# Routing's order from the last unit but one on, and the weights of both expert layers through four common buffers

## The chip, the core and the metric

The kernel runs on one core of one Trainium2 chip. The metric is the device time of one execution in microseconds (us). Differences are read against the kernel before on the same chip. The core has TensorE (PE, with its weight load PEld), VectorE (DVE), ScalarE (ACT), GpSimd (POOL) and SyncE (SP). In this kernel SP issues nearly all transfers, POOL issues a few, and nothing but SP and POOL issues any.

## The reference, cut to what matters

```python
# x, ctx: (4, 1024, 512) f32; 16 heads of 32
x = x + attention(layernorm(x), ctx, ctx)      # causal mask, softmax, @ Wo.T + bo
n = layernorm(x)                               # the tokens of the second part
grouped = n.reshape(4, 32, 32, 512)            # groups g of 32 tokens t
logits = einsum('bgtd,des->bgtes', grouped, controller) + tie      # 32 x 4 = 128 experts
perm = (logits == max(logits, over t))         # each expert takes one token of each group
disp = einsum('bgtd,bgtes->bgesd', grouped, perm)
inner = relu(einsum('bgesd,desf->bgesf', disp, f1) + bias)         # first layer
y = einsum('bgesf,esfd->bgesd', inner, f2)                         # second layer
x = x + einsum('bgesd,bgtes->bgtd', y, perm)
```

## The kernel before, in words

**Attention.** 16 units (4 batches times 4 chunks of 128 hidden columns, four heads each) run one after the other. Unit `u` has 12 steps `k`. In step `k` the scores of unit `u+1` are formed for their row maxima (`score_piece`, L426, reduced by DVE in L438), and the scores of unit `u` are formed transposed (`key_block`, L492 and L498), exponentiated by ACT (L506), masked by POOL (`affine_select`, L509), summed by DVE and POOL (L525 to L529) and multiplied with the values (`weigh_values`, L542). The sums are gathered on PE (`pd`, L572) and inverted (L579). All but the last inverse go to DRAM and come back spread over the partitions (L583, L586), and L567 multiplies them in. The output product of a batch (`o_step`, L374, with the addition L379) runs in later units. The order is written by a planner: `fill` and `soon` hold PE work, `slot` places it against estimated costs, and `later`/`beside` hold small DVE work, of which `beside(0.9)` takes some in each step. PE, DVE, ACT and POOL execute in the order of this source (`manual_schedule`); SP too in the units after the first. In routing and in the expert layers, SP is left to the scheduler.

**Routing.** The 4096 tokens go through in eight blocks `q` of 512 tokens (four rows of 128). Blocks 0 to 5 belong to batches 0 to 2 and are read back from `x2_dram` (`load_tokens`, 1 MB each). Blocks 6 and 7 are the last batch, whose eight output rows are made here: `last_row` loads the residual, adds the output bias on POOL (`residual`, L344), forms the product in the one buffer of `ps_o` (L911), adds on DVE (L916), stores, and measures the row (L362, L363). A block is normalized (`normalize_row`, L737, four rows, in place), stored to `xn_dram`, turned by PE (`turn_row`, L748), multiplied with the controller (`choose_tokens`, L930; DVE then adds `tie`, takes the maximum and compares, L937 to L942; POOL stores the choice, L944), turned back (`return_choice`, L949) and dispatched to the experts (`dispatch`, L1058, evicted by DVE L1066 and ACT L1068). Block 0 is turned inside the last unit (`turn_first`). Step `n` of the loop (L967) does: two turns of block `n`, the choice of block `n-1`, two turns, load of block `n+2`, normalization and store of block `n+1`, return of `n-2`, dispatch of `n-3`, then the rows of `LAST_ROWS[n-1]` (2, 2, 2, 1, 1, 0, 0).

**Expert layers.** The first layer takes four passes over chunks of 128 columns (`products`, L1115, added up in `inner`) beside the dispatch of the next chunk; its weights `f1` come in 16 transfers of 512 KB through four buffers. The second layer takes four passes `dq` of 128 output columns: eight `second_layer` steps `m` (L1183, weights `f2` in 32 transfers of 256 KB through twelve buffers), 32 turns (L1197), and in the next pass eight `combine` steps (L1208, L1212; loaded rows `xr` in eight buffers, stores issued by POOL in L1213).

The functions that the change touches, with the profile's line numbers:

Of the kernel before, what the change touches and what calls it, by code (L numbers as in the profile page):

```python
# [18 lines left out]
P = 128  # L19
# [5 lines left out]
def attention_phase(  # L25
# [696 lines left out]
    NQ = B * S // (QN * P)  # L722
    LAST = NQ - NT // QN
    LAST_ROWS = (2, 2, 2, 1, 1, 0, 0)
    xn_dram, permT_dram = routed
    tokens, turned = {}, {}

    def load_tokens(q):
        if q < LAST:
            tokens[q] = wpool.tile([P, QN, D], F32, tag=("w_q", "w_k")[q % 2], name=f"x2_{q}")  # L730
            nc.sync.dma_start(
                tokens[q], x2_dram[ts(q, QN * P), :].rearrange("(t p) d -> p t d", p=P)
            )
# [12 lines left out]
    def turn_row(q, i, px):  # L746
        for c in range(NC):
            nc.tensor.transpose(px[:, c, :], tokens[q][:, i, ts(c, P)], ident)  # L748

    def turn_first(i):  # L750
        finish(("rows", 0, i))
# [12 lines left out]
    for u in range(-1, NU):  # L764
# [129 lines left out]
    tie_sb = rpool.tile([P, T], F32, tag="tie", name="tie_sb", bufs=1)  # L894
    nc.sync.dma_start(tie_sb, tie)
    banks = ExitStack()
    ps_o = pool("ps_ro", 1, banks, space=PSUM)
    ps_x = pool("ps_rx", 2, banks, space=PSUM)
# [3 lines left out]
    def last_row(t):  # L902
        q, i = LAST + t // QN, t % QN
        if i == 0:
            tokens[q] = lpool.tile([P, QN, D], F32, tag="x2l", name=f"x2_{q}")
        if t + 1 < NT:
            load_residual(B - 1, t + 1)
        xt = residual(B - 1, t)
        po = ps_o.tile([P, D], F32, tag="po", name=f"po_{B - 1}_{t}")
        for c in range(NC):  # L910
            nc.tensor.matmul(  # L911
                po, lhsT=atTs[(B - 1) * NC + c][:, ts(t, P)], rhs=weights["o"][:, c, :],
                start=(c == 0), stop=(c == NC - 1),
            )
# [37 lines left out]
    def load_first(q):  # L952
# [2 lines left out]
            firsts[q], xn_dram[ts(q, QN * P), ds(0, P)].rearrange("(t p) d -> p t d", p=P)  # L955
        )

    firsts = {}

    for q in range(2):  # L960
        store_tokens(q)
    load_residual(B - 1, 0)
    variances((B - 2) * NT, (B - 1) * NT)
    roots((B - 2) * NT, (B - 1) * NT)
    load_tokens(2)
    row = 0
    for n in range(1, NQ):  # L967
        for i in range(2):
            turn_tokens(n, i)
        choose_tokens(n - 1)  # L970
        for i in range(2, QN):
            turn_tokens(n, i)
        load_tokens(n + 2)
        if 1 < n < LAST + 2:
            load_first(n - 2)
        if n + 1 < NQ:
            for i in range(QN):
                normalize_row(n + 1, i)
            store_tokens(n + 1)
        if n > 1:  # L980
            return_choice(n - 2)
        if n > 2:
            dispatch(n - 3, firsts.pop(n - 3))
        for _ in range(LAST_ROWS[n - 1]):
            last_row(row)
            row += 1
            if row % QN == 0:
                t = (B - 1) * NT + row
                variances(t - QN, t)
                roots(t - QN, t)  # L990
    first_layer.load_rows(1, 0)
    dispatch(NQ - 3, firsts.pop(NQ - 3))
    choose_tokens(NQ - 1)
# [78 lines left out]
def ffn_phase(ctx: ExitStack, tc, consts, x2_dram, routed, first_layer, f1, biasT, f2, out):  # L1072
# [20 lines left out]
    nc.sync.dma_start(bias_sb, biasT)  # L1093

    with first_layer.stack:
        f1pool = pool(first_layer.stack, "ffn_f1", 4, side="right")
# [6 lines left out]
        def load_f1(c, k):  # L1105
            f1k = f1pool.tile([P, 2 * QB * P], F32, tag="f1", name=f"f1_{c}_{k}")
            nc.sync.dma_start(f1k, f1[ts(c, P), ts(k, 2 * QB * P)])
            return f1k

        def products(c, disp, f1k, k):  # L1110
            pi = ps_i.tile([P, QB, G], F32, tag="pi", name=f"pi_{c}_{k}")
# [18 lines left out]
            if c == NC - 1:  # L1130
                nc.scalar.activation(part, part, AF.Relu)

        before = first_layer.disp
        order = {mybir.EngineType.PE, mybir.EngineType.DVE, mybir.EngineType.Activation}
        with tc.manual_schedule(engines=order):
            for c in range(1, NC + 1):
                if c < NC:
                    disp = first_layer.dispatched(c)
                for n in range(NK):
                    if c < NC:  # L1140
                        if n % 4 == 0:
                            xn = first_layer.load_rows(c, n // 4)
                        first_layer.dispatch(
                            c, n, lambda i, xn=xn, n=n: xn[:, n % 4 * 4 + i, :], disp
                        )
                    if n % 2 == 0:
                        f1k = load_f1(c - 1, n // 2)
                    products(c - 1, before, f1k, n)
                before = disp

    with ExitStack() as second:


        ytpool = pool(second, "ffn_yT", 1)
        xpool = pool(second, "ffn_x", 8)
        f2pool = pool(second, "ffn_f2", 12)
        ypool = pool(second, "ffn_y", 1)
        tpool = pool(second, "ffn_permT", 1, side="right")  # L1160
# [3 lines left out]
        nc.sync.dma_start(permT, permT_dram)  # L1164
        DQ, NM = f2.shape[0], f2.shape[1]
        DW = D // DQ
# [8 lines left out]

        def second_layer(dq, m, y):

            f2t = f2pool.tile([P, 4, DW], F32, tag="f2", name=f"f2_{dq}_{m}")
            nc.sync.dma_start(f2t, f2[dq, m])
            pys = [ps_y.tile([G, 4, DW], F32, tag="py", name=f"py_{dq}_{m}_{j}") for j in range(4)]  # L1180
            for i in range(4):
                for j in range(4):
                    nc.tensor.matmul(  # L1183
                        pys[j][:, i, :], lhsT=inner[ts(j, F), 4 * m + i, :],
                        rhs=f2t[ts(j, F), i, :], start=True, stop=True,
                    )
            for j in range(4):
                evict(
                    j == 0 or (j == 2 and dq == 0), y[:, :, ds(16 * m + 4 * j, 4)],
                    pys[j].rearrange("g i d -> g d i"),  # L1190
                )

        def turn(dq, k, y, yT):
# [3 lines left out]
                nc.tensor.transpose(pt[:, i, :], y[:, 4 * k + i, :], ident)  # L1197
            evict(k % 2 == 0, yT[:, :, ts(k, 4)], pt.rearrange("e i g -> e g i"))

        def combine(dq, a, yT):  # L1200

            xt = xpool.tile([P, 4, DW], F32, tag="xr", name=f"xr_{dq}_{a}")
            nc.sync.dma_start(xt, x2_v[a, :, :, ts(dq, DW)])
# [9 lines left out]
            nc.gpsimd.dma_start(out_v[a, :, :, ts(dq, DW)], xt)  # L1213

        yT = None
        order = {mybir.EngineType.PE, mybir.EngineType.DVE, mybir.EngineType.Activation}
        with tc.manual_schedule(engines=order):
            for dq in range(DQ + 1):
                before = yT
# [78 lines left out]
```

## Time and profile before

| | |
|---|---|
| times of three runs | 1463.23, 1463.23 and 1468.44 us; median 1463.23 us |
| the profiled execution | 1464.86 us, of which the span from first to last instruction is 1463.2 us |
| busy: PE, PEld, DVE, ACT, POOL | 1388.1, 718.0, 938.7, 502.7, 474.7 us |
| granted clock of TensorE, mean of the span | 0.990 |
| bytes moved | 120.53 MB, mean 82 GB/s |
| attention ends (last `pd`, L572) | about 1147.8 us |
| routing ends, first product of the first layer | about 1254 us |
| first layer ends, second layer begins | about 1323.5 us |

PE is busy for 95% of the span, so time is lost where PE stands idle or where its granted clock is below 1. The page's slices show both in the last quarter; the views of the trace in that quarter (chain of waits, timeline by engine) give the places. Times below are microseconds from the start of the span. In a timeline row the first number is the start, the second the length of the (merged) row, and the bracket says how long the engine stood idle before it and what released it.

### The profile page before, as it was taken

The numbers are of one execution on the slowest core, as the hardware profiler recorded it, in microseconds if no ns is written. First come the engines' busy times: TensorE is split into PE (matmuls) and PEld (weight loads), VectorE is DVE, ScalarE is ACT, GpSimd is POOL, SyncE is SP. The second block draws the span as 40 slices with busy tenths as digits, with TensorE's granted clock in tenths as the row PEclk, the third lists the DMA queues.
The fourth block names the chain that finished last, engine by engine and source line by source line (L and its number), as shares of the span: only waits on it lengthen the run. The fifth ranks groups of instructions, "written<-read, shape, count | busy, mean of one in ns | idle before, by whom it ended". The sixth has DMA issues, their size and how long they took to land.

```text
span 1463.2 us, 31732 instructions
## 1 busy us (share of the span) xinstructions
PE 1388.1 (95%) x13710; PEld 718.0 (49%) x13710; DVE 938.7 (64%) x1391; ACT 502.7 (34%) x791; POOL 474.7 (32%) x554
## 2 busy tenths in 40 slices
PE   6999999999999999999999999999998889897997
PEld 4533444344453533444445344434443345787887
DVE  3567767775656576755657666555667557576665
ACT  1033323333223223232223232323234214645664
POOL 1024443342424253434353434342443211000122
PEclk9999999999999999999999999999999899999999
DMA  6002013010022101102122000110014565757654
GB/s 244 29 3 66 19 54 110 10 54 10 25 68 103 60 31 46 53 10 61 37 98 70 29 12 23 27 31 17 24 39 127 187 225 186 211 151 249 189 164 143
DMA packets 84076, 120.53 MB, mean 82 GB/s; under 512 B 6704, under 2 KB 42976, under 8 KB 83808
## 3 DMA queue, kind: packets, MB, share of 16 engines
q1 hardware_dynamic: 80736, 108.02, 23.2%
q0 software_dynamic: 3200, 10.49, 2.3%
q8 instruction: 107, 1.75, 0.5%
q14 instruction: 33, 0.27, 0.1%
HBM read 89.16 MB, written 29.32 MB: 81 GB/s over the span
## 4 chain that ended last, share of the span: by engine, by line
PE 72%; issue 14%; DVE 9%; POOL 2%; ACT 1%; DMA 1%; SPq 0%; POOLq 0%; DVEq 0%; ACTq 0%
PE sc L426 12%; PE st L492 10%; PE av L542 9%; PE pv L319 8%; PE pk L286 8%; PE pq L300 7%; PE po L374 6%; DVE nm L438 3%; PE sc L432 3%; PE st L498 2%; PE po L911 2%; PE pl L930 2%; PE pd L572 2%; POOL out_dram L1213 2%; DVE xnT L252 1%
## 5 line engine op out<-in xcount | busy, mean ns | idle before, releaser
L438 DVE TENSOR_REDUCE nm<-sc 128x2 f32<-128x1024 f32 (+3 forms) x384 | 349.4, 951 | 293.9 <-PE sc L432 193.3
L506 ACT ACTIVATE pr<-st 128x1024 f32<-128x1024 f32 (+3 forms) x384 | 290.4, 808 | 571.3 <-PE st L498 524.6
L509 POOL TENSOR_SCALAR_AFFINE_SELECT pr<-pr 128x256 f32<-128x256 f32 x256 | 124.0, 493 | 419.6 <-ACT pr L506 417.7
L529 POOL TENSOR_TENSOR acc<-acc,pr 128x512 f32<-128x512 f32 (+1 forms) x120 | 194.4, 1620 | 82.0 <-ACT pr L506 72.7
L426 PE MATMUL sc<-kT,qT 32*128 32x512 f32 (+3 forms) x1536 | 205.7, 533 | 10.3 <-ACT pr L506 6.9
L492 PE MATMUL st<-qT,kT 32*128 32x512 f32 (+3 forms) x1536 | 192.7, 536 | 0.4 <-DVE nm L438 0.2
L542 PE MATMUL av<-pr,v 128*32 128x512 f32 (+3 forms) x1536 | 164.8, 500 | 0.7 <-ACT raw L555 0.4
L286 PE MATMUL pk<-ct,w_k 128*128 128x512 f32 x256 | 131.7, 633 | 9.6 <-DMA w_k<-in_wkT_dram 9.2
L300 PE MATMUL pq<-xnT,w_q 128*128 128x512 f32 x256 | 129.5, 620 | 7.7 <-DVE xnT L252 6.3
L319 PEld LDWEIGHTS pv<-w_v,ct 128*128 128x128 f32 x1024 | 120.6, 193 | 32.3 <-issue 24.9
L319 PE MATMUL pv<-w_v,ct 128*128 128x128 f32 x1024 | 132.0, 282 | 0.0
L492 PEld LDWEIGHTS st<-qT,kT 32*128 32x128 f32 x1536 | 68.6, 184 | 128.4 <-issue 101.2
L529 DVE TENSOR_TENSOR acc<-acc,pr 128x1024 f32<-128x1024 f32 (+3 forms) x136 | 127.8, 944 | 4.1 <-POOL pr L509 4.1
L426 PEld LDWEIGHTS sc<-kT,qT 32*128 32x128 f32 x1536 | 74.2, 183 | 113.8 <-issue 56.8
L526 POOL TENSOR_TENSOR acc<-pr,pr 128x768 f32<-128x768 f32 (+1 forms) x30 | 62.5, 2084 | 172.8 <-ACT pr L506 172.8
L374 PE MATMUL po<-w_o,atT 128*128 128x512 f32 x192 | 94.8, 614 | 1.3 <-DVE rd L579 1.1
L1213 POOL DMA_DIRECT2D out_dram<-xr x32 | 24.0, 752 | 184.8 <-DVE xr L1212 184.6
L286 PEld LDWEIGHTS pk<-ct,w_k 128*128 128x128 f32 x256 | 44.2, 194 | 69.8 <-issue 55.9
L498 PE MATMUL st<-mxT,ones 32*128 32x512 bf16 (+3 forms) x768 | 73.7, 321 | 0.7 <-DVE mxT L469 0.7
L300 PEld LDWEIGHTS pq<-xnT,w_q 128*128 128x128 f32 x256 | 42.2, 189 | 62.0 <-issue 44.9
L542 PEld LDWEIGHTS av<-pr,v 128*32 128x32 f32 x1536 | 31.4, 108 | 82.9 <-issue 68.0
L1197 PE MATMUL pt<-ident,y 128*128 128x128 f32 x512 | 56.7, 273 | 3.3 <-ACT y L1174 2.0
(108 smaller groups left out, 1480.7 us busy)
## 6 DMA issues: line engine op xcount, KB each, us to landing
ct<-in_ctxT_dram SPq DMA_DIRECT2D x8, 1024.0 KB, 5.5
xt<-in_x_dram SPq DMA_DIRECT2D x8, 1024.0 KB, 6.1
xr<-in_x_dram SPq DMA_DIRECT2D x32, 256.0 KB, 2.7
xn_dram<-x SPq DMA_DIRECT2D x8, 1024.0 KB, 5.1
f<-in_f_dram SPq DMA_DIRECT2D x16, 512.0 KB, 4.7
f<-in_f_dram SPq DMA_DIRECT2D x32, 256.0 KB, 5.7
xr<-x_dram SPq DMA_DIRECT2D x32, 256.0 KB, 4.2
out_dram<-xr POOLq DMA_DIRECT2D x32, 256.0 KB, 3.8
```

The lines of the kernel that those rows point to most:

```text
L286: nc.tensor.matmul(pk, lhsT=weights["k"][:, c, ts(hc, P)], rhs=cts[b, half][:, c, :], start=(c == 0), stop=(c == NC - 1),)
L300: nc.tensor.matmul(pq, lhsT=weights["q"][:, c, ts(hc, P)], rhs=xnTs[b][:, c, ts(half, HS)], start=(c == 0), stop=(c == NC - 1),)
L319: nc.tensor.matmul(pv[:, t, :], lhsT=cts[b, half][:, c, ts(t, P)], rhs=weights["v"][:, c, ts(hc, P)], start=(c == 0), stop=(c == NC - 1),)
L374: nc.tensor.matmul(po, lhsT=atTs[b * NC + c][:, ts(t, P)], rhs=weights["o"][:, c, :], start=(c == 0), stop=(c == NC - 1),)
L426: nc.tensor.matmul(scs[r // 2][:, r % 2, :n], lhsT=qT[rr, ts(i, P)], rhs=kT[rr, ds(c0, n)], start=True, stop=not diag,)
L438: nc.vector.tensor_reduce(nm[:, c0 // HS, i % 4, ts(g, 2)], scs[g][:, :, :n], AX.X, ALU.max, negate=True)
L492: nc.tensor.matmul(scs[r // 2][:, r % 2, :n], lhsT=kT[rr, ts(j, P)], rhs=qT[rr, ds(h * HS + q0, n)], start=True, stop=False,)
L498: nc.tensor.matmul(scs[r // 2][:, r % 2, :n], lhsT=ones16[rr, :], rhs=mxT[rr, ds(q0, n)], start=False, stop=True,)
L506: nc.scalar.activation(pr[:, :, :n], scs[g][:, :, :n], AF.Exp)
L509: nc.gpsimd.affine_select(out=d, in_=d, compare_op=ALU.is_ge, fill=0.0, base=0 if j == 0 else -1, pattern=[[0, 2], [P + 1, P]], channel_mu ...
L529: engine.tensor_tensor(acc, acc, pr[:, :, :n], ALU.add)
L542: nc.tensor.matmul(avs[u, h][rr, q0:], lhsT=vs[u][:, j, rr], rhs=pr[r // 2][:, r % 2, : HS - q0], start=(j == 0), stop=(j == last),)
```

## The change

It has two parts. In the first, the loads of blocks 0 and 1 and their normalization go from the last unit to the last but one (steps 5 and 8); the small table `tie` is loaded in the last unit; the bias is added on POOL for the last batch's first rows ahead of time (`prepare_row`, two of them inside the last unit, the rest at the start of a step); a loop step normalizes the next block first and then makes one of its rows between the turns and the choice and the other at its end; block 3 is loaded into the buffer `w_v`. In the second, the weights of both expert layers come in pieces of 512 KB through one pool of four buffers, the next piece being asked for when one is used up; SP joins the engines that run in the source's order, and the loads of `xn`, `xr` and `permT` are written where they shall be issued.

```diff
@@ attention_phase
     def load_tokens(q):
         if q < LAST:
-            tokens[q] = wpool.tile([P, QN, D], F32, tag=("w_q", "w_k")[q % 2], name=f"x2_{q}")
+            tag = "w_" + "qkqvkq"[q]
+            tokens[q] = wpool.tile([P, QN, D], F32, tag=tag, name=f"x2_{q}")
...
+    def prepare_row(t):
+        if t < NT and t not in prepared:
+            if (B - 1, t) not in residuals:
+                load_residual(B - 1, t)
+            prepared[t] = residual(B - 1, t)
...
-            if u == NU - 1 and k == 0:
+            if u == NU - 2 and k == 5:
                 load_tokens(0)
                 load_tokens(1)
-                for q in range(2):
-                    for i in range(QN):
-                        later(("wait rows", q, i), 0.4, lambda: None)
+            if u == NU - 2 and k == 8:
                 for q in range(2):
                     for i in range(QN):
                         later(("rows", q, i), 0.5, lambda q=q, i=i: normalize_row(q, i))
...
+                tie_sb = wpool.tile([P, 2 * T], F32, tag="mask_first", name="tie_sb")[:, :T]
+                nc.sync.dma_start(tie_sb, tie)
+                for t in range(2):
+                    prepare_row(t)
+                load_residual(B - 1, 2)
                 add("turn", 0, [turn_first(i) for i in range(QN)], 4 * SMALL)
...
     for n in range(1, NQ):
+        rows = LAST_ROWS[n - 1]
+        for t in range(row, row + rows + 1):
+            prepare_row(t)
+        if n > 1:
+            normalize_tokens(n + 1)
         for i in range(2):
             turn_tokens(n, i)
+        if rows > 1:
+            next_row()
         choose_tokens(n - 1)
+        if n == 1:
+            normalize_tokens(n + 1)
+            load_tokens(3)
         for i in range(2, QN):
             turn_tokens(n, i)
-        load_tokens(n + 2)
+        if n < 3:
+            load_tokens(n + 3)
         if 1 < n < LAST + 2:
             load_first(n - 2)
-        if n + 1 < NQ:
-            for i in range(QN):
-                normalize_row(n + 1, i)
-            store_tokens(n + 1)
         if n > 1:
             return_choice(n - 2)
         if n > 2:
             dispatch(n - 3, firsts.pop(n - 3))
-        for _ in range(LAST_ROWS[n - 1]):
-            last_row(row)
...
+        if rows:
+            next_row()
@@ ffn_phase
+    order = {
+        mybir.EngineType.PE, mybir.EngineType.DVE, mybir.EngineType.Activation, mybir.EngineType.SP
+    }
...
+    wpool = pool(ctx, "ffn_w", 4, side="right")
...
+    def load_weights(n):
+        w = wpool.tile([P, 8 * P], F32, tag="w", name=f"w_{n}")
+        if n < 4 * NC:
+            c, k = divmod(n, 4)
+            nc.sync.dma_start(w, f1[ts(c, P), ts(k, 8 * P)])
+        else:
+            dq, k = divmod(n - 4 * NC, NM // 2)
+            w = w.rearrange("p (m i d) -> p m i d", m=2, i=4)
+            nc.sync.dma_start(w, f2[dq, ts(k, 2)].rearrange("m p i d -> p m i d"))
+        weights.append(w)
...
                     if n % 2 == 0:
-                        f1k = load_f1(c - 1, n // 2)
+                        f1k = weights.popleft()
                     products(c - 1, before, f1k, n)
+                    if n % 2 == 1:
+                        next_weights()
...
-            f2t = f2pool.tile([P, 4, DW], F32, tag="f2", name=f"f2_{dq}_{m}")
-            nc.sync.dma_start(f2t, f2[dq, m])
+            f2t = weights[0][:, m % 2]
...
                         second_layer(dq, m, y)
+                        if m % 2 == 1:
+                            weights.popleft()
+                            next_weights()
                     if dq:
                         combine(dq - 1, m, before)
+                        if m < NM - 1:
+                            load_x()
+                    elif m == 1:
+                        nc.sync.dma_start(permT, permT_dram)
...
                         turn(dq, k, y, yT)
+                        if k % 4 == 3 and (dq == 0 or k == 3):
+                            load_x()
```

More of the change, by code (lines that the diff above doesn't have):

```diff
@@ L724, in attention_phase @@
     LAST_ROWS = (2, 2, 2, 1, 1, 0, 0)
+    assert LAST == 6
     xn_dram, permT_dram = routed
@@ L748, in turn_row @@
             nc.tensor.transpose(px[:, c, :], tokens[q][:, i, ts(c, P)], ident)
+    prepared = {}
+    def prepare_row(t):
[3 more added lines that the diff above has]
+            prepared[t] = residual(B - 1, t)
     def turn_first(i):
@@ L893, in attention_phase @@
     lpool = pool("route_last", 2)
-    tie_sb = rpool.tile([P, T], F32, tag="tie", name="tie_sb", bufs=1)
-    nc.sync.dma_start(tie_sb, tie)
     banks = ExitStack()
@@ L905, in last_row @@
             tokens[q] = lpool.tile([P, QN, D], F32, tag="x2l", name=f"x2_{q}")
-        if t + 1 < NT:
-            load_residual(B - 1, t + 1)
-        xt = residual(B - 1, t)
+        xt = prepared[t]
         po = ps_o.tile([P, D], F32, tag="po", name=f"po_{B - 1}_{t}")
@@ L956, in load_first, with normalize_tokens @@
         )
+    def normalize_tokens(q):
+        if q < NQ:
+            for i in range(QN):
+                normalize_row(q, i)
+            store_tokens(q)
     firsts = {}
@@ L961, in attention_phase @@
         store_tokens(q)
-    load_residual(B - 1, 0)
     variances((B - 2) * NT, (B - 1) * NT)
@@ L966, in attention_phase, with next_row @@
     row = 0
-    for n in range(1, NQ):
+    def next_row():
+        nonlocal row
+        last_row(row)
+        row += 1
+        if row + 2 < NT:
+            load_residual(B - 1, row + 2)
+        if row % QN == 0:
+            t = (B - 1) * NT + row
+            variances(t - QN, t)
+            roots(t - QN, t)
+    for n in range(1, NQ):
+        rows = LAST_ROWS[n - 1]
[3 more added lines that the diff above has]
+            normalize_tokens(n + 1)
         for i in range(2):
             turn_tokens(n, i)
+        if rows > 1:
+            next_row()
         choose_tokens(n - 1)
+        if n == 1:
+            normalize_tokens(n + 1)
+            load_tokens(3)
         for i in range(2, QN):
             turn_tokens(n, i)
-        load_tokens(n + 2)
+        if n < 3:
+            load_tokens(n + 3)
         if 1 < n < LAST + 2:
             load_first(n - 2)
-        if n + 1 < NQ:
-            for i in range(QN):
-                normalize_row(n + 1, i)
-            store_tokens(n + 1)
         if n > 1:
@@ L983, in attention_phase @@
             dispatch(n - 3, firsts.pop(n - 3))
-        for _ in range(LAST_ROWS[n - 1]):
-            last_row(row)
[L986 to L990, printed above, removed]
+        if rows:
+            next_row()
     first_layer.load_rows(1, 0)
@@ L1093, in ffn_phase, with next_weights @@
     nc.sync.dma_start(bias_sb, biasT)
+    wpool = pool(ctx, "ffn_w", 4, side="right")
+    DQ, NM = f2.shape[0], f2.shape[1]
+    DW = D // DQ
+    weights = deque()
+    def load_weights(n):
[8 more added lines that the diff above has]
+        weights.append(w)
+    for n in range(4):
+        load_weights(n)
+    loads = iter(range(4, 4 * NC + DQ * NM // 2))
+    def next_weights():
+        for n in loads:
+            load_weights(n)
+            return
     with first_layer.stack:
-        f1pool = pool(first_layer.stack, "ffn_f1", 4, side="right")
         first_layer.xpools.append(pool(first_layer.stack, "ffn_rows_more", 2))
@@ L1103, in ffn_phase @@
         QB = NQ // NK
[L1105 to L1108, printed above, removed]
         def products(c, disp, f1k, k):
@@ L1131, in products, with load_rows @@
                 nc.scalar.activation(part, part, AF.Relu)
+        rows = iter([(c, half) for c in range(1, NC) for half in range(2)])
+        def load_rows():
+            for c, half in rows:
+                first_layer.load_rows(c, half)
+                return
+        for _ in range(3):
+            load_rows()
         before = first_layer.disp
-        order = {mybir.EngineType.PE, mybir.EngineType.DVE, mybir.EngineType.Activation}
         with tc.manual_schedule(engines=order):
@@ L1140, in ffn_phase @@
                     if c < NC:
-                        if n % 4 == 0:
-                            xn = first_layer.load_rows(c, n // 4)
+                        xn = first_layer.load_rows(c, n // 4)
                         first_layer.dispatch(
@@ L1145, in ffn_phase @@
                         )
+                        if n % 4 == 3:
+                            load_rows()
                     if n % 2 == 0:
-                        f1k = load_f1(c - 1, n // 2)
+                        f1k = weights.popleft()
                     products(c - 1, before, f1k, n)
+                    if n % 2 == 1:
+                        next_weights()
                 before = disp
@@ L1157, in ffn_phase @@
         xpool = pool(second, "ffn_x", 8)
-        f2pool = pool(second, "ffn_f2", 12)
+        tpool = pool(second, "ffn_permT", 1)
         ypool = pool(second, "ffn_y", 1)
-        tpool = pool(second, "ffn_permT", 1, side="right")
         ps_y = pool(second, "ps_y", 6, space=PSUM)
@@ L1163, in ffn_phase @@
         permT = tpool.tile([ES, N], F32, tag="permT", name="permT")
-        nc.sync.dma_start(permT, permT_dram)
-        DQ, NM = f2.shape[0], f2.shape[1]
-        DW = D // DQ
         x2_v = x2_dram.rearrange("(a t p) d -> a p t d", p=P, t=4)
@@ L1198, in turn, with load_x @@
             evict(k % 2 == 0, yT[:, :, ts(k, 4)], pt.rearrange("e i g -> e g i"))
+        xts = deque()
+        rows = iter([(dq, a) for dq in range(DQ) for a in range(NM)])
+        def load_x():
+            for dq, a in rows:
+                xt = xpool.tile([P, 4, DW], F32, tag="xr", name=f"xr_{dq}_{a}")
+                nc.sync.dma_start(xt, x2_v[a, :, :, ts(dq, DW)])
+                xts.append(xt)
+                return
         def combine(dq, a, yT):
-            xt = xpool.tile([P, 4, DW], F32, tag="xr", name=f"xr_{dq}_{a}")
-            nc.sync.dma_start(xt, x2_v[a, :, :, ts(dq, DW)])
+            xt = xts.popleft()
             po = ps_o.tile([P, 4, DW], F32, tag="po", name=f"po2_{dq}_{a}")
@@ L1215, in ffn_phase @@
         yT = None
-        order = {mybir.EngineType.PE, mybir.EngineType.DVE, mybir.EngineType.Activation}
         with tc.manual_schedule(engines=order):
```

## The prediction

> **What bounds the kernel now.** I read the page's slices first: PE is full up to slice 30 of 40 and not after it, and slice 32 (1134 to 1170 us) alone has a lower granted clock.
>
> ```profile
> PE   6999999999999999999999999999998889897997
> PEclk9999999999999999999999999999999899999999
> ```
>
> So the change acts where PE has holes. The chain of waits for that stretch (start, length, what) says who fills them:
>
> ```profile
> 1129.23 2.11 issue
> 1131.34 0.97 PE px L748 x4
> 1132.32 1.87 PE av L542 x8
> ...
> 1157.87 4.85 DVE x L737 x4
> 1163.37 6.49 PE po L911 x8
> ...
> 1179.94 0.99 DVE x L737 x2
> 1181.59 5.40 PE po L911 x8
> ...
> 1198.09 1.20 DVE disp L1066 x2
> 1199.94 5.28 PE po L911 x8
> ...
> 1212.07 3.63 PE po L911 x8
> ```
>
> Four times PE waits for DVE, and the eight products after a hole take 5.28 to 6.49 us instead of 3.45 (two chain rows show 3.45 and 3.63 without a hole). In PE's timeline the holes are 3.91, 5.88, 2.54 and 2.47 us. Three times the cause is one order on DVE: the addition that frees the only bank of `ps_o` (L916) stands behind four normalizations (L737). The windows of 10 us show the granted clock beside it:
>
> ```profile
> 1160.00:1170.00 10.00, 6.63 (x11) 2.96 (x12) 4.22 (x7) 0.00 (x0) 1.51 (x2) 0.66 0.57 192
> 1170.00:1180.00 10.00, 9.05 (x35) 4.67 (x33) 7.26 (x9) 2.67 (x5) 3.05 (x3) 1.00 0.52 173
> ```
>
> (last three columns: clock, DMA share, GB/s.) After a hole PE runs at about half rate for some 4 us. Where the length of a hole decides this is open: 2.47 us was followed by it, 2.33 us (1318.7) and 1.42 us were not. [...]
>
> How long four normalizations take is told by POOL's rows beside them:
>
> ```profile
> 1157.87 4.85 DVE L737 TENSOR_SCALAR x<-x,moments,rstd 128x512 f32<-128x512 f32 x4
> 1211.62 3.45 DVE L737 TENSOR_SCALAR x<-x,moments,rstd 128x512 f32<-128x512 f32 x4
> 1232.59 1.91 DVE L737 TENSOR_SCALAR x<-x,moments,rstd 128x512 f32<-128x512 f32 x4
> ...
> 1159.03 2.48 POOL L344 TENSOR_TENSOR xr<-xr,bo_sb 128x512 f32<-128x512 f32 x2
> 1212.58 1.28 POOL L344 TENSOR_TENSOR xr<-xr,bo_sb 128x512 f32<-128x512 f32 x1
> ```
>
> With no bias addition 1.91, with one 3.45, with two 4.85: the two engines exclude each other, and one normalization (0.54 alone) has waited up to 3.48 us.
>
> **Part 1a, routing proper.** I count from T, the end of the last `pd` (1147.83). PE's work is the same; its order changes.
> - Row 0's product now stands ahead of `pl` 0, so `pl` no longer covers the wait for `pb` and `atT`. From the rows: inverse 0.96, copies 0.56, `pb` 0.86, L567 0.69; the two turns cover 0.9. PE idles about 0.6 + 0.9: **+1.5**.
> - Row 1 then comes after `pl` 0 and two turns (3.45 + 0.9 us after row 0), and its bank was freed 0.7 us after row 0. The hole of 5.88 and its half rate (6.49 - 3.45 = 3.04) go: **-8.9**.
> - Late next: DVE does the three steps on `pl` 0 (0.7 each) to T+12.4, then four normalizations of block 2 beside one bias addition (3.45) to T+15.8, then row 1's addition to T+16.5. Row 2's product could start at T+15.4: **+1.0**, too short for half rate. Bounds: 0 (normalizations at 1.91) to 2.5 + 1.9 (at 4.85, as in the hole at 1179). I take one bias addition, since row 4's load is issued only after row 1's addition.
> - Rows 3 and 5: now each comes a `pl`, two turns and a return (3.45 + 0.9 + 0.6) after the row before it; the normalizations, up to 4.85, run beside the other row. The holes 2.54 + (5.40 - 3.45) and 2.47 + (5.28 - 3.45) go: **-4.5, -4.3**. DVE's load per step (3.45 + 2.1 + 1.4 + two rows at 1.6 = 10.2) stays below PE's 12.7 to 13.8. **+0.5** for `pl`'s single bank, read late where DVE is behind (0 to 1.5).
> - Loads: block 3 waits for the buffer `w_v`, so for `pl` 0 (T+10.3), and lands 6.2 later (median of `x<-x_dram`); DVE wants it at T+17.4, and row 2's addition behind it has 4 us of slack. Blocks 4 and 5 have over 8 us. Row 3's addition waits only for its bias; those loads land in 2.9 us. SP still holds them between stores; each store is ready before the load behind it is wanted. `tie`'s wait (4.41 us on DVE) goes; it was inside the 5.88.
>
> Sum: 1.5 - 8.9 + 1.0 - 4.5 - 4.3 + 0.5 = **-14.7** (-17 to -8).
>
> **Part 1b, the last two units.** Eight normalizations, two loads of 1 MB, two stores of 1 MB, three bias additions and `tie` come in here.
> - The first turn no longer waits for the normalization behind L567: 3.91 goes, with the half rate after it (px 0.35, av 0.87, st 0.36): **-5.5**.
> - DVE now does four normalizations of block 1 between 1105 and 1112, ahead of L379. That addition is already late there:
>
> ```profile
> 1112.43 0.38 PE L464 MATMUL pmx<-ident,mxs 128*128 128x128 bf16 x4 [0.78 <-DVE xr L379]
> ```
>
>  L379 frees the bank for `pmx`. The first normalization fits an idle stretch of 1.71 us on DVE; three are added in front, 1.6, and behind them or between them masks (0.41) and a bias addition (1.26) of POOL: +3.2 on L379, and PE's hole of 0.78 becomes 4.0, with 1.6 of half rate: **+4.8**. Bounds: 0 (all fit) to 6.5 (each meets a POOL operation).
> - The bias additions of rows 0 to 2 stand ahead of the masks of step 8 on POOL. Their loads are queued on SP behind the last inverse (issue ends 1128.40) and two small loads, so from about 1129.3, and land by 1132. Three at 1.27, in turn with two sums on DVE (1.22 each, from 1131), end near X + 9.7, X being the end of step 7's scores (1127.43). The masks then take 0.41; the values of step 8 start at X + 9.9, where PE's own work would allow X + 5.8: **+4.1** (0 to 5.8, with half rate).
> - From there to the last `pd`, DVE loses seven normalizations (3.3 us; 8.8 of 10 us were busy); masks and sums in turn remain: **-1.5** (0 to -2.5).
> - The 1 MB loads follow the read-backs that end 1062.5 and take 6.2 each, so the next inverse (store 1070.13) is late by at most 1 us; L567 there has 2.8 (1078.53 against 1073.6 + 2.1). The stores pass near 1098 and 1114, the next read-back has 1.6 of slack, and behind it DVE alone would wait: 0.
>
> Sum: **+1.9** (-5 to +8).
>
> **Part 2, the expert layers.** The built orders show the same PE order, and in the first layer SP's order is the one it had. What differs is the pass boundary: before, ten transfers of `f2` start from 1308.9; now a piece starts only when two `products` have freed its buffer. Such a step pair takes 2.0 us, so the first `f2` piece starts at F + 2.2 (F = 1313.4), lands some 4.7 later (median of 512 KB) and is wanted at F + 8.3; the next ones have 2 to 4 us of slack, since a pair of second-layer steps takes 3.5 us. In the later passes four pieces free up within a pass, each wanted a pass later, with 14 us of turns between; SP waits for POOL's store (3.8 to landing) ahead of each `xr`, a constant lag at a pace of 2.12. Nothing is late: 0. Fewer bytes in flight at the boundary may shorten this hole in the middle of a step, for which the trace names no releaser:
>
> ```profile
> 1321.03 2.59 PE L1115 MATMUL pi<-disp,f 128*32 128x128 f32 x82 [2.33 <-issue]
> ```
>
> Bounds 0 and -2.3; the first layer's three others (1.0 to 1.4) came with fewer bytes in flight, so **-1.0**.
>
> **Total**: -14.7 + 1.9 - 1.0 = -13.8. The profiled execution took 1464.86 (span 1463.2), so 1451.1 there; it is 1.6 above the median shown, so against the median 1463.23 the forecast is **1449.4**.
>
> **Rivals.**
> - *The units cost nothing* (16%): normalizations find DVE's idle time and the bias additions end before the masks. For: DVE is 64% busy. Against: both stand in front in the built order. Without 4.8 and 4.1: 1440.5.
> - *The row's wait stays* (14%): the addition that frees `ps_o` still follows four normalizations in each step; if these meet two bias additions and PE arrives earlier than I count, rows 2 and 4 wait as rows 3 and 5 did, 2 x 4.4: 1458.2. That is also about what a change that doesn't do what it says would give.
> - *DVE and POOL block each other in the last units* (8%), the slower side: between 1084 and 1148, eight normalizations each wait for one whole POOL sum (2.35 + 0.54, together 23.1), and three bias additions each for a DVE sum (1.27 + 1.22, together 7.5). All of it on PE is 30.6 where I count 8.9: +21.7, so 1471.1. It decides from 22.7 us of new holes there. For: L379 already holds PE. Against: PE waits for DVE only at `pmx` and at `pd`.
> - My forecast has the remaining 62%.
>
> [...]
>
> **Numbers.** The range takes in the bounds of the last units and most of the second rival: 1441 to 1460. A difference below 0.5% (7.3 us) can't be told from none. Faster 0.62 + 0.16 = 0.78; same 0.14 (second rival); slower 0.08.
>
> **What would show it.** In the changed profile: no hole above 1.5 us before a row's product (else the second rival); a hole of 3 to 5 us before `pmx` near 1112, and one of 3 to 4 before the values of step 8, with POOL's three bias additions just before it (else the first); four normalizations beside one bias addition in the first loop step; the second layer starting without a wait for `w`. I am wrong if a transfer ends a wait of PE, or if holes appear in the passes after 1338.

## The result, and the profile after

The changed kernel takes 1448.59 us (median of four: 1444.81, 1448.30, 1448.88, 1449.10) where the kernel before takes 1463.23: ratio 0.9885, 95% interval 0.9858 to 0.9911. Run again beside the last experiments it took 1449.39 us, ratio 0.9901 (0.9885 to 0.9916). The forecast was 1449.4.

The profiled execution is the fastest of the four, 1444.81 us with a span of 1443.1. Its slices (PE's busy share and granted clock):

```profile
PE   6999999999999999999999999999998899898997
PEclk9999999999999999999999999999999999999999
```

The single 8 of the clock row is gone, and the slices of routing are full. The chain of waits shows the same stretch:

```profile
1155.02 3.56 DVE x L739 x4
1159.23 3.70 PE po L921 x8
1162.93 3.43 PE pl L940 x8
1166.36 0.87 PE px L750 x8
1167.80 3.44 PE po L921 x8
1171.24 0.87 PE px L750 x8
1172.11 3.68 PE po L921 x8
```

One wait for four normalizations is left in it, and no product of a row (L921) takes longer than 3.7 us, where 5.28 to 6.49 stood before. In the windows of 10 us PE is busy throughout at full clock, with a DMA share of 1.05 and 0.87 beside it:

```profile
1160.00:1170.00 10.00, 10.00 (x33) 5.05 (x32) 6.21 (x11) 1.59 (x3) 1.77 (x2) 1.00 1.05 392
1170.00:1180.00 10.00, 10.00 (x35) 5.02 (x33) 6.79 (x13) 1.38 (x3) 3.83 (x4) 1.00 0.87 299
```

PE's timeline has the two holes that the prediction named in the last unit, one small one before row 2, and the one between the expert layers, now 0.70 instead of 2.33:

```profile
1110.23 0.38 PE L464 MATMUL pmx<-ident,mxs 128*128 128x128 bf16 x4 [2.89 <-DVE xr L379]
1134.40 1.41 PE L542 MATMUL av<-pr,v 128*32 128x512 f32 x8 [2.99 <-POOL pr L509]
1159.23 3.70 PE L921 MATMUL po<-w_o,atT 128*128 128x512 f32 x8 [0.79 <-DVE x L926]
1300.39 2.38 PE L1168 MATMUL pi<-disp,w 128*32 128x128 f32 x76 [0.70 <-issue]
```

Cutting each kernel's PE timeline at the same events tells where the time went. M is the start of the scores in unit 14 that wait 0.74 us for ACT (1074.17 before), T the end of the last `pd`, R the end of row 7's product, F the first product of the first layer (the prediction's F is the start of that layer's last pass). Half rate is the state in which PE's granted clock is 0.50 (from 1164 to 1169 us of the kernel before) and a matmul takes up to 1.9 times as long (there 6.49 us instead of 3.45 for the eight products of a row). The medians were measured in several sessions, with 1462.87 to 1464.08 for the kernel before beside them, so kernels are compared by their ratio. All in us:

| kernel | median | ratio to before, 95% | to M | M to T | T to R | R to F | F to end |
|---|---|---|---|---|---|---|---|
| before | 1463.23 | | 1074.17 | 73.66 | 78.36 | 27.84 | 209.17 |
| changed | 1448.59 | 0.9858 to 0.9911 | 1069.86 | 72.64 | 63.87 | 28.13 | 208.60 |
| changed_again | 1449.39 | 0.9885 to 0.9916 | 1071.68 | 74.77 | 63.87 | 28.13 | 207.75 |
| weights_only | 1460.49 | 0.9968 to 0.9989 | 1071.37 | 73.80 | 78.59 | 27.85 | 208.39 |
| routing_only | 1452.12 | 0.9910 to 0.9934 | 1071.28 | 73.94 | 63.88 | 28.13 | 213.27 |
| rows_together | 1448.74 | 0.9887 to 0.9915 | 1074.50 | 72.60 | 64.20 | 28.13 | 206.97 |
| norm_mid | 1447.69 | 0.9883 to 0.9909 | 1074.73 | 73.50 | 63.87 | 27.85 | 208.55 |
| together_mid | 1448.54 | 0.9874 to 0.9921 | 1074.83 | 73.53 | 64.04 | 27.84 | 207.86 |
| bias_in_rows | 1446.92 | 0.9860 to 0.9911 | 1074.24 | 69.93 | 65.08 | 28.13 | 207.62 |
| tie_early | 1452.35 | 0.9903 to 0.9948 | 1071.36 | 70.34 | 74.80 | 27.84 | 205.26 |
| f2_four | 1464.29 | 0.9995 to 1.0025 | 1072.46 | 74.52 | 63.87 | 28.13 | 222.32 |
| w_burst | 1453.73 | 0.9909 to 0.9953 | 1074.27 | 74.01 | 63.88 | 28.13 | 212.31 |
| packed_in_rows | 1445.52 | 0.9857 to 0.9890 | 1072.36 | 70.82 | 65.10 | 28.13 | 206.89 |
| both_moved | 1441.24 | 0.9832 to 0.9872 | 1072.56 | 67.71 | 63.88 | 28.14 | 207.21 |

The spans differ by 20.1 us: 14.49 between T and R (routing), 1.02 in the last two units, 0.57 in the expert layers, -0.29 in the last dispatch, and 4.31 ahead of M, where both kernels run the same code: there the profiled execution of before had a lower clock at 60 to 70 and at 505 to 515 us (0.83 in the mean of either stretch), that of the changed kernel had none (1.00). So about 4 us of the 20 belong to this pair of profiles and not to the change, which the medians (14.6 apart) say too.

### The profile page after: what moved, and what is told of

Its sections match the earlier page's. It is cut to its first block, busy times and chain, and to the rows that moved or that the text cites. A ratio compares the mean times of both kernels' runs of the same rounds, so it can differ in the third digit from the quotient of the medians.

```text
span 1443.1 us, 31676 instructions
## 1 busy us (share of the span) xinstructions
PE 1377.2 (95%) x13710; PEld 714.1 (49%) x13710; DVE 934.0 (65%) x1391; ACT 502.9 (35%) x791; POOL 477.7 (33%) x554
## 4 chain that ended last, share of the span: by engine, by line
PE 72%; issue 14%; DVE 9%; POOL 2%; ACT 1%; DMA 1%; SPq 0%; POOLq 0%; DVEq 0%; ACTq 0%
PE sc L426 12%; PE st L492 10%; PE av L542 9%; PE pv L319 8%; PE pk L286 8%; PE pq L300 7%; PE po L374 6%; DVE nm L438 3%; PE sc L432 3%; PE st L498 2%; PE po L921 2%; PE pd L572 2%; POOL out_dram L1279 2%; DVE xnT L252 1%; PE pl L940 1%
```

## Experiments

**Each part alone.** routing_only takes the changed kernel with the whole of `ffn_phase` as before (its pools below), weights_only the reverse:

```diff
-    wpool = pool(ctx, "ffn_w", 4, side="right")
...
+        f1pool = pool(first_layer.stack, "ffn_f1", 4, side="right")
...
+        f2pool = pool(second, "ffn_f2", 12)
```

> The changed order of the last two units and of routing, with the expert layers' loads as they were before. Theory (the time comes from routing's order on DVE): about 14 to 15 us below the kernel before, so 1448.6 to 1449.5, and the stretch from the last sums to the end of row 7's product 78.4 - 14.5 = 63.9 us long, as in the changed kernel. Rival (the common weight buffers bring a good part of it, through less traffic beside routing): only half of it, about 1456.

> The expert layers' loads through four common buffers with SyncE in the source's order, with routing as before. Theory: 0 to -1 us (the holes in the middle of expert steps for which no releaser is shown, 5.9 us before and 5.4 after, stay): 1462 to 1463. Rival: about 1456, with the holes before row 1, 3 and 5 shorter although their order on DVE is unchanged.

Measured 1452.12 and 1460.49, 11.4 and 3.0 us below 1463.5, the median of before beside them. Routing's stretch T to R is 63.88 in the one and 78.59 in the other, so routing's gain is all from the first part. But the second part is worth about 3 us (1.6 to 4.7 by the interval), not 0 to 1, and so both times missed their ranges; its rival's 7 is excluded as well. Part of it lies between the layers, in PE's timelines of routing_only (two rows) and of weights_only (the third):

```profile
1297.87 5.46 PE L1144 MATMUL pi<-disp,f 128*32 128x128 f32 x180 [0.21 <-ACT disp L1097]
1306.48 3.87 PE L1144 MATMUL pi<-disp,f 128*32 128x128 f32 x76 [3.15 <-issue]
...
1316.45 2.59 PE L1139 MATMUL pi<-disp,w 128*32 128x128 f32 x82 [0.63 <-issue]
```

In routing_only there is a hole of 3.15 us, and 3.87 instead of 2.38 for the 76 products behind it (granted clock 0.53 from 1306 to 1309 us); F to the end is 4.67 longer than in the changed kernel. From before to weights_only the hole falls from 2.33 to 0.63, without half rate behind either, and F to the end by only 0.78, since weights_only fell to half rate in the turns of the first pass (15.83 instead of 14.16 us).

**Which edit of the loop.** rows_together makes both rows of a step at its end again; norm_mid puts the normalizations back into the middle of every step.

```diff
 # rows_together
-        if rows > 1:
-            next_row()
         choose_tokens(n - 1)
...
-        if rows:
+        for _ in range(rows):
             next_row()
 # norm_mid
-        if n > 1:
-            normalize_tokens(n + 1)
...
             load_first(n - 2)
+        normalize_tokens(n + 1)
```

> The changed kernel, but both rows of a step again stand one behind the other at its end; the normalizations stay where the change put them: in the first step between the first choice and the rows, as before, in the second and third step at the head. Theory (a row waits since the addition that frees the only bank stands behind four normalizations): before row 1 a hole of 4 to 6 us comes back, before rows 3 and 5 only the turn of the bank, about 1 us; together 6 to 10 us above the changed kernel, 1455 to 1459. Rival (two rows one behind the other on one bank are the cause, wherever the normalizations stand): holes of 5.9, 2.5 and 2.5 us in all three, 1460 to 1464.

> The changed kernel, but in every step the four normalizations stand in the middle, behind the choice, as before; the rows stay split, one ahead of the choice and one at the end. Theory (split rows alone suffice: the row at the end comes late enough for its addition, and its bank is free): 0 to 3 us above the changed kernel, 1448 to 1452, no hole above 1.5 us before a row's product. Rival (their place is what matters): a hole of 2 to 3 us before rows 2 and 4, which follow a row whose addition stands behind the normalizations, about 1455.

norm_mid came as its theory said. rows_together did not: before row 1 both its theory and its rival expected a long hole to come back, and T to R grew by only 0.33 us (1448.74 instead of 1455 or more). My theory, that a row waits because its addition stands behind four normalizations, had missed something: before row 1 the order on DVE was that of before, and the hole was 0.78, because the four normalizations took 1.91 us there and not 4.85.

**What runs beside the normalizations.** So the next three kernels undo both edits (together_mid), only the early additions of `bo` (bias_in_rows), and all three (tie_early, where of routing's changes only the early loads, `tie`'s among them, stay).

```diff
 # together_mid = rows_together + norm_mid
 # bias_in_rows
-                for t in range(2):
-                    prepare_row(t)
-                load_residual(B - 1, 2)
+                for t in range(3):
+                    load_residual(B - 1, t)
...
-        xt = prepared[t]
+        xt = residual(B - 1, t)
...
-        for t in range(row, row + rows + 1):
-            prepare_row(t)
 # tie_early = together_mid + bias_in_rows
```

> The changed kernel with both edits of the routing loop's order undone: rows one behind the other at the end of a step, normalizations in the middle of every step, as before. What stays of the change there is that the additions of bo (L344) are made a step ahead of their rows and that tie is loaded in the last unit. New theory (a row waited because the four normalizations met the additions of bo on POOL, 4.7 to 4.85 us instead of 1.9, and because the first choice waited for tie): holes before rows 1, 3 and 5 of 0.8 to 1.5 us, no bias addition beside the normalizations, 1448 to 1450.5. Rival (split rows and early normalizations each suffice alone, and with both undone the holes come back): 3 us or more before row 1 and 2.5 before rows 3 and 5, 1455 or more.

> The changed kernel, but each row's addition of bo on POOL is made with the row again, as before, instead of a step ahead; the loops' new order and the early load of tie stay. New theory (what counts is what runs beside the normalizations): in the first steps the normalizations meet additions of bo again and take 3.5 to 4.9 us; with split rows the wait is smaller than it was, holes of 1 to 3 us before rows 2 and 4, 1449 to 1453. Rival (the new order alone is the gain): as the changed kernel, 1448 to 1449, and no hole above 1 us.

> Routing's order as before (rows together, normalizations in the middle, additions of bo with their rows), with the changed kernel's last two units, its early load of tie and its expert layers. New theory: the first choice begins about 2.6 us earlier (1155.81 before, when pl was there at 1153.2), so the hole before row 1 falls from 5.88 to about 3.3 us, and those before rows 3 and 5 stay at 2.5; about 7 us of holes above the changed kernel, and half rate behind some of them: 1454 to 1460. Rival (tie's wait lay inside another one): 5.9, 2.5 and 2.5, and 1460 or more.

PE's and DVE's timelines of together_mid:

```profile
1158.80 3.70 PE L921 MATMUL po<-w_o,atT 128*128 128x512 f32 x8 [0.78 <-DVE x L926]
1172.70 3.70 PE L921 MATMUL po<-w_o,atT 128*128 128x512 f32 x8 [1.01 <-DVE x L926]
1187.74 3.70 PE L921 MATMUL po<-w_o,atT 128*128 128x512 f32 x8 [0.85 <-DVE x L926]
...
1155.80 1.91 DVE L739 TENSOR_SCALAR x<-x,moments,rstd 128x512 f32<-128x512 f32 x4
```

and of tie_early:

```profile
1154.65 5.40 PE L920 MATMUL po<-w_o,atT 128*128 128x512 f32 x8 [3.29 <-DVE x L925]
1171.78 5.40 PE L920 MATMUL po<-w_o,atT 128*128 128x512 f32 x8 [2.54 <-DVE x L925]
1190.14 5.40 PE L920 MATMUL po<-w_o,atT 128*128 128x512 f32 x8 [2.48 <-DVE x L925]
...
1149.14 4.85 DVE L739 TENSOR_SCALAR x<-x,moments,rstd 128x512 f32<-128x512 f32 x4
```

The order on PE and DVE is the same in these two; what differs is whether POOL adds `bo` beside the normalizations (two additions beside the 4.85, none beside the 1.91; in the second step of together_mid they overlap in part, and the four take 2.85). That is the whole difference of 74.80 - 64.04 = 10.8 us between T and R. And bias_in_rows, with the additions beside the normalizations but the new order, has 65.08: before a row's product nothing above 0.85, and one hole of 1.44 before a turn, here with the normalizations ahead of it:

```profile
1156.61 4.86 DVE L739 TENSOR_SCALAR x<-x,moments,rstd 128x512 f32<-128x512 f32 x4
...
1160.70 0.63 PE L750 MATMUL px<-ident,x 128*128 128x128 f32 x4 [1.44 <-DVE x L739]
```

So new theory and the rivals were each half right: **the new order and the early additions each suffice alone, to within 1.2 us**, since the one takes away who waits and the other what is waited for. Having both is no gain in the changed kernel: the early additions save these 1.2 us of T to R, and M to T is 2.7 longer with them (72.64 against 69.93); in time the two kernels are not told apart.

`tie`'s early load is worth 78.36 - 74.80 = 3.6 us. The first choice on DVE waits for the table in the kernel before, and for its product in tie_early; counted from T it begins 2.59 us earlier there, and the hole before row 1 falls by the same 2.59, from 5.88 to 3.29, as expected:

```profile
1155.81 0.69 DVE L937 TENSOR_TENSOR lg<-pl,tie_sb 128x512 f32<-128x512 f32 x1 [4.41 <-DMA tie_sb<-in_tie_dram]
...
1147.09 0.69 DVE L946 TENSOR_TENSOR lg<-pl,tie_sb 128x512 f32<-128x512 f32 x1 [1.82 <-PE pl L939]
```

tie_early's 1452.35 is below its expected 1454, since without additions ahead of the masks its last unit is also shorter (M to T 70.34).

**The hole between the layers.** f2_four is routing_only with `pool(second, "ffn_f2", 4)` in place of 12. w_burst adds copies to the changed kernel:

```diff
                     if n % 2 == 1:
                         next_weights()
+                    if c == NC and n in (4, 5):
+                        for i in range(4):
+                            nc.sync.dma_start(
+                                burst[ds(4 * n - 16 + i, 1)], x2_burst[ds(4 * n - 16 + i, 1)]
+                            )
```

> The routing_only kernel (changed routing, expert layers as before), but the second layer's weights in four buffers instead of twelve, so that fewer transfers start at the boundary between the layers. Theory (the hole in the middle of the last step of the first layer is a fetch of PE's instructions through the same DMA engines, and is long where these are full): a hole of 0.6 to 1.5 us there in place of the 3.15 in routing_only and 2.33 before, and 1449 to 1451. Rival (it has nothing to do with the transfers): 2.3 to 3.2 us again, 1452.

> The changed kernel with 2 MB more traffic at the boundary between the expert layers: eight copies of 256 KB from DRAM to DRAM, which nothing reads, issued by SyncE in steps 4 and 5 of the first layer's last pass. Theory (the hole in the middle of that pass's last steps is a fetch of PE's instructions that shares the DMA engines): the hole behind the 180th product grows from 0.70 to 2 to 3.5 us, with no releaser named, at the same place. Rival (the hole has another cause): 0.6 to 0.9 us as in the changed kernel; waits for w may come in either case.

In f2_four the hole at the same place is 0.92:

```profile
1305.25 2.38 PE L1144 MATMUL pi<-disp,f 128*32 128x128 f32 x76 [0.92 <-issue]
```

The 76 products behind it run at full rate again (2.38 us), and with four buffers the hole is 0.92 where twelve had 3.15, so its length goes with the transfers. (The kernel as a whole became slower, 222.32 from F to the end, because PE then waited 9.2 us for `f2` in five steps; my expected time had left that out.) In w_burst the copies were issued only at 1304.17, behind pieces of `w` that had to wait for their buffers, and the hole that ends at 1305.91 stayed at 0.70: the copies came too late to test it, since its instruction packet (see below) had ended at 1304.63. But a hole of 1.23 came 127 products later, in the middle of a step, while the copies ran. In packed_in_rows a hole of 0.41 stands behind the same product (the last row); the other profiles have none there:

```profile
1310.21 0.77 PE L1250 MATMUL py<-w,inner 32*128 32x128 f32 x15 [0.61 <-DVE y L1240]
1312.22 1.07 PE L1250 MATMUL py<-w,inner 32*128 32x128 f32 x17 [1.23 <-issue]
1313.64 2.09 PE L1250 MATMUL py<-w,inner 32*128 32x128 f32 x32 [0.35 <-DVE y L1240]
...
1306.56 0.73 PE L1237 MATMUL py<-w,inner 32*128 32x128 f32 x17 [0.41 <-issue]
```

Behind the hole of 1.23 four steps ran at about half rate (1.95 to 2.09 instead of 1.17, granted clock 0.50 from 1315 to 1320 us). What the engine lacks in such a hole is suggested by the DMA queues of routing_only from 1303 to 1306.5 us (packets, MB, share of the 16 engines):

```profile
q1 hardware_dynamic: 760, 1.34, 101.4%
q8 instruction: 1, 0.02, 1.7%
```

The profile counts an instruction queue among those of the 16 engines, with one packet of 0.02 MB in this hole, and the data's packets beside it take 101.4% of the engines' time. With the changed routing the hole stands behind the 180th product of the pass whichever way the weights are loaded (routing_only, f2_four, changed), with the old routing behind the 174th (before, weights_only), and with three other orders of routing behind the 173rd, 181st and 175th (norm_mid, rows_together, together_mid): the place goes with the program ahead of it, the length with the traffic (3.15 and 2.33 us with twelve buffers for `f2`, at most 0.92 with four).

The times of the single packets in the traces say more than these sums. The 14 profiles have 72 holes of more than 0.2 us in the middle of a group of equal matmuls for which no releaser is named. Each of them, from 0.22 to 3.15 us long, ends 1.20 to 1.61 us behind the end of a packet of the instruction queue, while these packets lie some 3 to 14 us apart in the expert layers. In routing_only the packet ends at 1305.03 and PE goes on at 1306.48. No releaser names the packet, but so fixed a distance leaves little else for PE to wait for. The packet's length doesn't tell the holes apart: it takes 0.98 us there, and 0.95 for the hole of 0.70 in the changed kernel. That it starts late there, and that full DMA engines are why, no run showed; f2_four (0.92 instead of 3.15) and w_burst (1.23 beside the copies) speak for it, one profile each.

**The two steps of the last units.** both_moved takes away what the prediction had priced at 4.8 and 4.1; packed_in_rows is bias_in_rows with the first of its edits.

```diff
-                        later(("rows", q, i), 0.5, lambda q=q, i=i: normalize_row(q, i))
+                        later(("rows", q, i), 0.2, lambda q=q, i=i: normalize_row(q, i))
+            if u == NU - 1 and k == 5:
+                for t in range(2):
+                    load_residual(B - 1, t)
+            if u == NU - 1 and k == 7:
+                for t in range(2):
+                    prepare_row(t)
...
-                for t in range(2):
-                    prepare_row(t)
                 load_residual(B - 1, 2)
...
     beside(1e9)
+    prepare_row(2)
     ordered.close()
```

> The changed kernel with the two steps in the last units moved that had cost PE a hole: the eight normalizations are planned at 0.2 instead of 0.5 us each, so that all stand ahead of unit 14's last maxima and none ahead of L379; rows 0 and 1 are loaded three steps earlier and their additions of bo stand in step 7, where POOL is idle, and row 2's stands behind the last masks. Theory (these two were the price of the units): the hole before pmx falls from 2.89 to about 0.8 us, the one before the values of step 8 from 2.99 to 0 to 0.7; 4 to 5 us below the changed kernel, 1443.5 to 1444.5. Rival (DVE and POOL have no free place there, and the waits come back as late maxima, late sums before the last pd or a late inverse): 1447 or more, with new holes between 1085 and 1148.

> bias_in_rows with the eight normalizations packed as in both_moved; the additions of bo stay with their rows, so only row 0's stands in the last unit. Theory: the hole before pmx goes from 2.89 to about 0.8, the hole of 1.44 before the turns of block 2's successor stays; 2 us below bias_in_rows, 1444.5 to 1445.5, and about the same as both_moved. Rival: as bias_in_rows, 1447.

In both_moved the wait before `pmx` is back at 0.78, and the largest one from there to T is 0.61:

```profile
1112.17 0.38 PE L464 MATMUL pmx<-ident,mxs 128*128 128x128 bf16 x4 [0.78 <-DVE xr L379]
...
1139.86 0.41 PE L572 MATMUL pd<-acc,pick 128*32 128x128 f32 x4 [0.61 <-DVE acc L529]
```

M to T is 67.71, 4.93 below the changed kernel's first profile and 7.06 below its second, which has half rate behind both holes; in time it is 1441.24 against 1449.39 beside it, the best of all kernels here and below the expected 1443.5. packed_in_rows did not gain its 2 us: its 1.4 in time lie within the intervals, and M to T is 0.89 longer than in bias_in_rows (70.82 against 69.93). The hole before `pmx` did fall to 0.78, but one of 1.61 before the values of step 8 stands in it that bias_in_rows had not.

**The clock, once more.**

> The changed kernel itself, once more, beside the last three. 1447 to 1450 us. Theory (whether PE falls to half rate behind a short wait is chance, not a matter of the wait's length): the same holes before 1050 us as in the first profile (0.95, 0.94, 1.93, 0.95, 1.25, 0.95), but half rate behind one or two of them, where the first profile had none; each such fall costs 1.5 to 1.7 us. Rival (the length of the hole decides): no half rate before 1050 again, and 1445.

The same wait of 0.95 us near 995, in the first profile of the changed kernel and in the second:

```profile
994.67 0.49 PE L426 MATMUL sc<-kT,qT 32*128 32x128 f32 x4 [0.95 <-ACT pr L506]
995.09 0.40 PE L432 MATMUL sc<-mask_strict,ident 128*128 128x128 bf16 x4
995.32 2.00 PE L319 MATMUL pv<-w_v,ct 128*128 128x128 f32 x16
```

```profile
994.90 0.49 PE L426 MATMUL sc<-kT,qT 32*128 32x128 f32 x4 [0.95 <-ACT pr L506]
995.32 0.40 PE L432 MATMUL sc<-mask_strict,ident 128*128 128x128 bf16 x4
995.56 3.22 PE L319 MATMUL pv<-w_v,ct 128*128 128x128 f32 x16
```

Same code, same wait, and 2.00 against 3.22 us for the same 16 products (granted clock 1.00 and 0.66 from 995 to 1000 us). Of the six holes before 1050 us this one alone was followed by half rate in the second profile, and none in the first, as the theory expected. This place had half rate in 6 of the 14 profiles; behind the hole of 2.9 before `pmx` it came in 5 of 10 and cost 1.5 to 1.6 us; behind those of 2.47 to 2.54 in routing in 6 of 6. In these profiles the length alone does not decide.

## Why the prediction was right, point by point

- **1a, routing, -14.7: -14.49.** The terms came too, most of them within 0.5 us. Row 0 idles 0.21 at `pb` and 0.85 at its product (+1.5 forecast); rows 1, 3 and 5 have no hole and no half rate (-8.9, -4.5, -4.3); row 2's product waits 0.79, behind four normalizations of 3.64 us with one addition beside them (+1.0 forecast, from 3.45). No half rate followed it (3.70 us), but "too short for half rate" rested on one hole of 1.42 us: near 995 us a wait of 0.95 was followed by it in 6 of the 14 profiles. The rows:

```profile
1154.93 3.64 DVE L739 TENSOR_SCALAR x<-x,moments,rstd 128x512 f32<-128x512 f32 x4
...
1156.09 1.28 POOL L344 TENSOR_TENSOR xr<-xr,bo_sb 128x512 f32<-128x512 f32 x1
```

- **Its reason was too narrow.** "Three times the cause is one order on DVE": together_mid keeps that order and has no such hole. The cause was that order together with POOL's additions beside the normalizations and, in the first step, `tie`. The forecast did not depend on this, since the change took away both the order and most of the additions beside the normalizations. And "tie's wait goes; it was inside the 5.88" is borne out: it was 2.6 of the 5.88.
- **1b, last units, +1.9: -1.0 in the first profile, +1.1 in the second,** and -1.1 to +0.9 in the six other profiles with the same last units. The first turn's wait went (-4.0 from `pmx` to the first turn). The step that was wrong is L379, **+4.8**, of which 3.2 was idle time and 1.6 half rate: it delayed `pmx` by 2.1, since the four normalizations took 4.2 us on DVE there and its idle stretches of 1.71 and 0.30 took up the rest, and half rate followed in only half of the profiles. The additions ahead of the masks, +4.1, cost 17.34 - 13.47 = 3.9 from the first turn to T (changed against tie_early; 3.6 for routing_only, which like tie_early fell to half rate behind `pmx`). That they run in turn with two sums (2 x 1.22 of the term) was the author's estimate and no run shows it: the three took 3.71 us back to back, and the sums were done by then. DVE's relief, -1.5, is about -1.8: from the first turn to T tie_early is 3.0 shorter than before, of which 1.23 is the half rate behind the first turn's wait.
- **Part 2, -1.0.** The place was right (the hole without a releaser at the boundary, 2.33, is 0.70 now), the size was not: 3 us in time. The hole reaches 3.15 us with the old loads, and half rate can follow it (1.5 us in routing_only, none in the profile of before); how often it does so in before no profile tells, so the rest of the 3 us is not placed. The second layer begins without a wait for `w`, as forecast, and no wait of PE is ended by a transfer there.
- **The sum was right partly by luck, because two of its errors cancel**: the last units were counted some 1 to 3 us too dear, the weights about 2 us too cheap.
- **Rivals.** "The units cost nothing" gave 1440.5; both_moved, which takes their two prices away, reads 1441.24: the prices were real in the changed kernel, though so close a number has the cheaper weights in it too. "The row's wait stays" would have needed POOL's additions beside the normalizations and the old order, which is tie_early. "DVE and POOL block each other" in the last units: the new holes there are 2.1 and 3.0, far from 22.7. That each operation there waits for a whole one of the other engine was the author's estimate, and no run shows it; the kernel before has a mask of 1.02 us instead of 0.41 beside a sum on DVE (1137.98). The two holes that the forecast named came just below its marks: 2.89 for 3 to 5, 2.99 for 3 to 4.

## What to carry to other kernels

When an engine's work stands behind a group of DVE operations, ask first what POOL does beside that group: moving small additions out of its way took 10.8 us here, reordering the loop 9.7, and either made the other nearly superfluous. In this kernel a wait of 1 to 3 us of PE is to be priced at itself plus a chance of some 1.6 us of half rate (6 of 14 profiles behind 0.95 us, 5 of 10 behind 2.9), so small holes are worth more than their length. PE can stop in the middle of a step without any wait in the program, here for up to 3.15 us beside a burst of transfers (routing_only, with a DMA share of 101.4% for data there): ask for weights piece by piece, but with enough buffers that none is late.

## What the runs showed of the hardware

Unexpected: T to R is reproduced to 0.01 us in six profiles of five kernels with the same order there (63.87 or 63.88), while code that no version touches, the stretch to M, varies by 5 us (1069.86 to 1074.83) between profiles. PE's matmuls up to M stand in the same order in all 14 profiles, and their waits of 0.9 us or more behind the first load are equal; against the changed kernel's first profile the others fall behind near 60 to 72, 270, 510 and 1000 us, where their granted clock is lower (before: 0.83 from 60 to 70 and from 505 to 515 us; both_moved: 0.80 from 260 to 265 and 0.69 from 995 to 1000) and its own is 1.00 (and by up to 1.1 us near 19 us, at a clock of 1.00). And the instruction queue in the DMA rows: the hole between the layers is at most 0.70 us in the eleven profiles with the four common buffers (in tie_early too short for a row), 0.92 in f2_four, and 2.33 and 3.15 in the two where `f2` has twelve.
